# Two-head half-key attention slots, single products and output eighths, weight sums on VectorE, and a ring of query columns in a paged-attention kernel

## The chip, the cores and the metric

The kernel runs on one core of a Trainium2 chip. The metric is the device time of one launch in microseconds, as a median over runs. The engines are TensorE (PE; its weight loads are PEld), VectorE (DVE), ScalarE (ACT), GpSimd (POOL), and SyncE (SP), whose queue issues most of the DMA transfers.

## The reference

Two residual layers follow each other. The first is a 32x32 mix of the sequence rows of each batch, chosen by a condition. The second is paged attention with grouped heads. All is float32.

```python
B, S, HID = 64, 32, 512          # batches, new tokens of each, width
D, HQ, HK = 128, 32, 8           # head width, query heads, key/value heads
PAGES, PSIZE, NPP = 64, 32, 16   # cache pages, tokens of a page, pages of a batch

x = x + einsum('bct,bcd->bdt', x, weights[condition])          # layer 1

q, k, v = x @ Wq.T, x @ Wk.T, x @ Wv.T                         # layer 2, by heads
q, k = rope(rmsnorm(q, q_norm_w), pos), rope(rmsnorm(k, k_norm_w), pos)
k_all = concat([k_cache[block_table], k]); v_all = concat([v_cache[block_table], v])
scores = q @ k_all.T / sqrt(D)       # 512 cached keys (valid where < cache_seqlens), 32 new
o = softmax(scores) @ v_all          # four query heads share a key/value head
x = x + o @ Wo.T
```

## The kernel before

The work is 32 steps. Steps 0 to 15 are the sixteen groups of four batches (BT = 4, that is 128 rows) for the first four key/value heads, steps 16 to 31 the same groups for the other four. A step `n` runs over its four batches `bt` and, in each, over four slots `g`. So it has sixteen slots, `slot = bt * 4 + g`. In a slot of the kernel before, one key/value head `g` of one batch is worked on, with its four query heads times 32 tokens as 128 columns and all 512 cached keys.

In every slot TensorE computes the `scores` (L828: four 128x128 products), ScalarE makes the exponentials (L839), and TensorE computes the `values` of the slot before (L889: four 128x129 products, the last column being the sum of weights). After each second head VectorE adds the new tokens' part (L907), takes the reciprocal (L909) and scales into a tile `o` (L910); `turn` (L920) transposes it in 32x32 blocks into `ot`. VectorE copies the keys of a head from their pages into `kh` (`head_keys`, L821), `KH` = 3 slots ahead. SP loads the sixteen key pages of a batch (`load_k`, L321), two batches ahead. GpSimd gathers the values, one chunk of 128 keys at a time, by indirect DMA into one of three `raw` tiles (`fetch`, L348), and ScalarE copies them, scaled by 0 or 1 for validity, into the value tile (`mask_v`, L361).

At the head of a step come the new tokens' own scores (`new_scores`: L849, exponentials `pn` L857) in slot 0 and their values (`new_values`: L873, copied by ScalarE into `nv`, L881) in slots 1 and 3.

Between these a plan, written out by hand, puts pieces of work at (step, slot):

- The projections. From step 4 on, the q, k and v of two steps (a `Pair`, `s0` even and `s1` odd) are made together while the two steps before them run, by a scheme with seven products instead of eight (`products`, L687). A set `k` covers two projection blocks; sets 0 and 2 are made in the even step, set 1 in the odd one. Each set comes in four pieces (`p1_p6`, `p5_p2`, `p3_p7`, `p4_last`), two products in a piece but the last. The scheme needs sums of weights: `sums_w` and `sums_w4` make them on VectorE (L656 to L667) for the first pair of each half, store them to DRAM as `sums_d`, and `load_sums` (L674) brings them back for every later pair. The pieces add with VectorE (L703) and hand each result to `finish`, which queues it.
- The norm of a queued result: `square_next` (ScalarE squares 512 columns, L465) and `norm_next` (VectorE: product with the rotation table L475, sum of squares L482, plus epsilon L483, two more products L489, add L495, scaling L497; GpSimd the power -1/2, L485), then `turn_rows` (VectorE transpose L517, GpSimd stores the row block to `heads_d`, L521). `norm_slots` lists the slots at which results are taken from the queue.
- `spread` (L530) brings a step's query and key columns back from `heads_d`, in four transfers for the first three batches (`q_cols`, one buffer) and four for the last (`q_last`, two buffers).
- The output projection of the step before (`out_proj`, L767): sixteen 128x512 products, in quarters, at slots 5, 7, 9 and 10 from step 4 on (`out_parts`).
- The inputs of a later pair (`x1_a` loads, `x1_c` mixes, `x1_b` transposes) in the first half; in the second half `load_x` brings back what was kept.

Product, output, new-token and mixing banks share four PSUM buffers (`pp`), scores have two, values two. On SP, TensorE and, in the whole of this run, on every engine, instructions stay in the order in which the program writes them. An instruction that waits therefore holds back all that stands behind it on its engine; SP's transfers too leave in program order.

Of the kernel before, what the change touches and what calls it, by code (L numbers as in the profile page):

```python
# [51 lines left out]
KH = 3  # L52
# [7 lines left out]
def cond_resid_paged_attention_kernel(  # L60
# [118 lines left out]
    def other_half(by):  # L179
# [10 lines left out]
        for kind in "qk"  # L190
    }
    sums_d = [
        [
            dram.tile([P, 3, 2 * 512], F32, tag=f"sums_d{hh}{k}", name=f"sums_d{hh}{k}")
            for k in range(3)
        ]
        for hh in range(NHH)
    ]
# [10 lines left out]
    def steps_of(exact, pools):  # L209
# [15 lines left out]
        else:  # L225
# [7 lines left out]
        v_bufs = [  # L233
            wpool.tile([P, VC, GH, D + 1], F32, tag=f"v{i}", name=f"v{i}_{uid}")
            for i in range(2)
        ]
# [7 lines left out]
        if exact:  # L244
            rows = wpool.tile([P, 4, GH + 1, P], F32, tag="rows", name=f"rows_{uid}")
        q_cols = wpool.tile([P, BT - 1, GH + 1, P], F32, tag="q_cols", name=f"q_cols_{uid}")
        q_last = [
            wpool.tile([P, GH + 1, P], F32, tag=f"q_last{i}", name=f"q_last{i}_{uid}")
            for i in range(2)
        ]  # L250
# [56 lines left out]
        def load_k(hh, b, first_pages):  # L307
            k_raw = kv.tile([P, NPP, GH, PSIZE], F32, tag="k_t", name=f"k_t_{hh}_{b}_{uid}")

# [10 lines left out]
            def load_page(j):  # L320
                ins = nc.sync.dma_start(  # L321
                    k_raw[:, j, :, :].rearrange("p g r -> p (g r)"),
                    kt[hh, bass.ds(page[j], 1)].rearrange("o d e -> (o d) e"),
                )
                if exact:
                    r, c = j % BT * PSIZE, j // BT
                    ins = nc.sync.dma_start(
                        v_bufs[b % 2][r : r + PSIZE, c, :, 0:D],
                        vc.rearrange("(p r h) (g d) -> p h r g d", r=PSIZE, h=NHH, g=GH)[
                            bass.ds(page[j], 1), hh  # L330
                        ].rearrange("o r g d -> (o r) g d"),
                    )
                last_k[:] = [ins.ins]

            for j in range(first_pages):
                load_page(j)
            return k_raw, [lambda j=j: load_page(j) for j in range(first_pages, NPP)]
# [20 lines left out]
        def mask_v(b, c, raw):  # L358

            ok = valid[:, b, c : c + 1]  # L360
            nc.scalar.activation(v_bufs[b % 2][:, c, :, 0:D], raw, AF.Copy, scale=ok)  # L361

        def mask_ones(b):
            nc.gpsimd.tensor_copy(
                v_bufs[b % 2][:, :, :, D], valid[:, b, :].unsqueeze(2).to_broadcast([P, VC, GH])
            )
# [8 lines left out]
        def x1_a(st):  # L375

            tag, bufs = "acc", 2 if exact else 1
            if 0 < st.n < 6 and not exact:
                tag, bufs = "sums", 2
            elif st.n and not exact:  # L380
                tag = ("u2", "u3")[st.n % 2]
# [81 lines left out]
        def squares(pp, name):  # L463
            sq = work.tile([P, 4, D], F32, tag="w2", name=f"sq_{name}", bufs=1)
            nc.scalar.activation(  # L465
                sq.rearrange("p h d -> p (h d)"), pp, AF.Square, scale=1.0 / math.sqrt(D)
            )
            return sq

        def norm_rope(st, pp, name, kind, sq, to=None):  # L470
# [10 lines left out]
            ms = small.tile([P, 4], F32, tag="ms", name=f"ms_{name}")  # L481
            nc.vector.tensor_reduce(ms, sq, AX.X, ALU.add)  # L482
            nc.vector.tensor_scalar_add(ms, ms, EPS)  # L483
            rs = small.tile([P, 4], F32, tag="rs", name=f"rs_{name}")
            nc.gpsimd.tensor_tensor(rs, ms, minus_half, ALU.pow)  # L485

# [21 lines left out]
        def columns(st, bt):  # L508
            return q_last[st.n % 2] if bt == BT - 1 else q_cols[:, bt]
# [13 lines left out]
        def spread(st, b0, b1):  # L523


            src = heads_d[st.n].rearrange("k (b d) i c -> k d b (i c)", b=BT)
            to = q_last[st.n % 2].unsqueeze(1) if b0 == BT - 1 else q_cols
            to = to.rearrange("p b i c -> p b (i c)")
            for k in range(4):
                nc.sync.dma_start(to[k * S : (k + 1) * S], src[k][:, b0:b1, :])  # L530
# [25 lines left out]
        def normed(st, i, pp, name, kind, sq):  # L556

            if by_tensor(st):
# [12 lines left out]
                norm_rope(st, pp, name, kind, sq, to)  # L571
            else:
                turn_rows(st, i, norm_rope(st, pp, name, kind, sq))

        def to_columns(st, i, copy=nc.scalar.copy):
# [3 lines left out]
            n = BT - 1  # L579
            copy(q_cols[:, :, i, :].rearrange("p b (h s) -> p b h s", h=4), p4[:, 0:n])  # L580
            copy(columns(st, n)[:, i, :].rearrange("p (h s) -> p h s", h=4), p4[:, n])
# [43 lines left out]
        def pair_x(pair):  # L625
            pair.x = work.tile([P, 7, 2, P], F32, tag="x", name=f"x_{pair.name}", bufs=1)
# [3 lines left out]
        def load_x(pair):  # L630
            for i, st in enumerate(pair.both):
                nc.sync.dma_start(st.x1t.rearrange("p c q -> p (c q)"), x1t_d[st.t])
# [18 lines left out]
        made = {}  # L651

        def sums_w(hh, k):


            b11, _, b12, b22 = halves(hh, k)  # L656
            nc.vector.tensor_tensor(b12, b12, b11, ALU.subtract)
            t2, t3 = (sums_tile(f"t{i}_{hh}{k}") for i in (2, 3))
            nc.vector.tensor_tensor(t2, b22, b12, ALU.subtract)
            nc.vector.tensor_tensor(t3, t2, b11, ALU.subtract)  # L660
            made[hh, k] = t2, t3

        def sums_w4(hh, k):
            for i, t in enumerate(made[hh, k]):
                nc.sync.dma_start(sums_d[hh][k][:, i, :], t)
            t2 = made[hh, k][0]
            nc.vector.tensor_tensor(t2, halves(hh, k)[1], t2, ALU.subtract)  # L667
            kept.append(lambda: nc.sync.dma_start(sums_d[hh][k][:, 2, :], t2))
            return t2

        def load_sums(pair, k, i):

            t = sums_tile(f"t{i + 2}_{pair.name}_{k}")
            nc.sync.dma_start(t, sums_d[pair.hh][k][:, i, :])  # L674
            pair.t[k, i] = t

        def products(pair, k, first, late_v):
# [5 lines left out]
            flat = lambda t: t.rearrange("p h d -> p (h d)")  # L683

            def product(bank, i, w, start=False):
                for c in range(2):
# [3 lines left out]
                        w[:, c * 512 : (c + 1) * 512],  # L690
# [17 lines left out]

            t = {}

            def p1_p6():
                t[2] = made[pair.hh, k][0] if first else pair.t[k, 0]
                b11, t["b21"], t[1], t["b22"] = halves(pair.hh, k)
                t["a"], t["b"] = bank("pa"), bank("pb")
                product(t["a"], A11, b11, True)
                t["z"] = temp("z")
                nc.scalar.copy(t["z"], t["a"])
                product(t["b"], S2, t[2], True)
                t["u2"] = temp("u2")
                add(t["u2"], t["b"], t["z"])  # L720
                if first:
                    t[4] = sums_w4(pair.hh, k)

            def p5_p2():
                t["c"] = bank("pc")
                product(t["c"], S1, t[1], True)
                t["u3"] = temp("u3")
# [409 lines left out]
        for pair in pairs:  # L1137
            pair.t = {}
# [329 lines left out]
```

## Time and profile before

| | |
|---|---|
| median of 3 runs | 2241.11 us (2234.92 to 2241.31) |
| profiled execution | 2247.31 us, span 2245.5 us |
| mean granted TensorE clock | 0.975 |
| DMA traffic | 479.18 MB, mean 213 GB/s |
| start of step 4, by its first `psn` record | 367.7 us |
| start of step 30 | 2125.7 us |

The profile is one execution. A busy time is the union of an engine's instructions. In a row of groups the columns are the line, engine, operation, output and inputs with their shapes, the count, the busy time and the mean of one in ns, then the idle time just before and what ended it. A row of waits has the waiting line, what released it, the total, the number of times and the longest. A row of the timeline has the start, the length, the instruction, and in brackets the idle time before it. A float32 matmul of 512 columns stands in the records as two, and so do the others but the transposes.

### The profile page before, as it was taken

To read this page: it belongs to the slowest core of one execution; us is meant where nothing else is said; L and a number is where in the kernel's file an instruction comes from. 1 tells how busy PE (TensorE), PEld (TensorE's weight loads), DVE (VectorE), ACT (ScalarE), POOL (GpSimd) and SP (SyncE) were. 2 spreads that over 40 slices of the span, in tenths; PEclk is the share of its full clock that TensorE was granted. 3 is DMA by queue.
4 is the path that set the end of the run, shared out by engine and by line. 5 is a ranking of instruction groups with operands and counts; after the bars stand their busy time and mean duration, and the time that the engine had idled before them with its cause. 6 is when DMAs were issued, how large, how long until landed. Compare 5 with 4: busy or idle time off the path is not lost.

```text
span 2245.5 us, 42014 instructions
## 1 busy us (share of the span) xinstructions
PE 2118.6 (94%) x12804; PEld 1491.4 (66%) x12804; DVE 1420.8 (63%) x3142; ACT 879.6 (39%) x1604; POOL 910.5 (41%) x1090
## 2 busy tenths in 40 slices
PE   7999888999999999898899989999999999999998
PEld 4766646676667667666566666766676676766675
DVE  5566665775657667576665656757576665667632
ACT  3444324343444424443234333434443344443442
POOL 3344444344444444443334443434434333444431
PEclk9999988999999999999999999999999999999999
DMA  8766656777777777788667987677777767777672
GB/s 250 186 179 189 173 168 207 221 213 219 214 229 227 216 221 210 224 274 250 188 197 233 252 251 215 203 218 224 225 225 225 214 199 227 235 222 224 199 203 86
DMA packets 424539, 479.18 MB, mean 213 GB/s; under 512 B 57104, under 2 KB 323728, under 8 KB 424304
## 3 DMA queue, kind: packets, MB, share of 16 engines
q1 hardware_dynamic: 366240, 291.99, 45.0%
q0 software_dynamic: 55168, 180.27, 26.6%
q10 hardware_dynamic: 2896, 4.14, 0.5%
q8 instruction: 105, 1.72, 0.3%
q14 instruction: 130, 1.06, 0.2%
HBM read 406.71 MB, written 69.47 MB: 212 GB/s over the span
## 4 chain that ended last, share of the span: by engine, by line
PE 70%; DMA 10%; DVE 5%; issue 5%; SPq 4%; POOL 3%; ACT 1%; DVEq 0%; POOLq 0%; ACTq 0%
PE pout_x L767 16%; PE po_x L889 15%; PE ps_x L828 15%; PE pb_x L687 8%; PE pc_x L687 6%; PE pa_x L687 6%; SPq L321 3%; DMA k_t_x<-in_kt_dram 3%; DMA raw_x<-in_vc_dram,v_row 3%; PE pp_q_x L458 1%; DMA t_x<-sums_d 1%; PE pnv_x L873 1%; POOL raw_x L348 1%; POOL rs_q_x L485 1%; PE psn_x L849 1%
## 5 line engine op out<-in xcount | busy, mean ns | idle before, releaser
L348 POOL DMA_INDIRECT raw_x<-in_vc_dram,v_row x512 | 517.7, 1011 | 458.8 <-ACT v_x L361 348.0
L889 PEld LDWEIGHTS po_x<-v_x,pr_x 128*128 128x128 f32 x4088 | 528.4, 194 | 178.0 <-issue 152.7
L839 ACT ACTIVATE pr_x<-ps_x 128x512 f32<-128x512 f32 x511 | 303.6, 594 | 725.9 <-PE ps_x L828 721.1
L889 PE MATMUL po_x<-v_x,pr_x 128*128 128x129 f32 x4088 | 560.5, 281 | 19.0 <-ACT pr_x L839 13.3
L767 PE MATMUL pout_x<-wo_x,ot_x 128*128 128x512 f32 x1024 | 459.4, 592 | 0.0
L828 PE MATMUL ps_x<-q_cols_x,kh_x 128*128 128x128 f32 x3064 | 417.2, 280 | 42.1 <-DVE rot_q_x L444 21.2
L821 DVE COPY kh_x<-k_t_x 128x512 f32<-128x512 f32 x506 | 214.2, 430 | 360.5 <-PE ps_x L828 171.8
L361 ACT ACTIVATE v_x<-raw_x,valid 128x512 f32<-128x512 f32 x512 | 365.8, 718 | 171.3 <-DMA raw_x<-in_vc_dram,v_row 166.9
L828 PEld LDWEIGHTS ps_x<-q_cols_x,kh_x 128*128 128x128 f32 x3064 | 384.3, 197 | 45.4 <-issue 44.6
L767 PEld LDWEIGHTS pout_x<-wo_x,ot_x 128*128 128x128 f32 x1024 | 186.5, 190 | 194.7 <-issue 194.6
L485 POOL TENSOR_TENSOR rs_q_x<-ms_q_x,minus_half 128x4 f32<-128x4 f32 x128 | 142.6, 1114 | 334.2 <-DVE ms_q_x L483 333.4
L521 POOL DMA_DIRECT2D heads_d<-rows_x x150 | 125.6, 838 | 311.2 <-DVE rows_x L517 258.7
L687 PE MATMUL pb_x<-t_x,x_x 128*128 128x512 f32 x432 | 203.5, 593 | 2.3 <-DMA t_x<-sums_d 1.3
L907 DVE TENSOR_TENSOR nv_x<-po_x,nv_x 128x258 f32<-128x258 f32 x256 | 106.1, 415 | 114.8 <-PE po_x L889 109.3
L687 PEld LDWEIGHTS pb_x<-t_x,x_x 128*128 128x128 f32 x432 | 79.0, 190 | 89.6 <-issue 83.5
L828 PE MATMUL ps_x<-q_last_x,kh_x 128*128 128x128 f32 x1024 | 136.0, 276 | 0.0
L828 PEld LDWEIGHTS ps_x<-q_last_x,kh_x 128*128 128x128 f32 x1024 | 125.5, 193 | 0.0
L910 DVE TENSOR_TENSOR o_x<-nv_x,rden 128x256 f32<-128x256 f32 x256 | 110.0, 430 | 8.7
L687 PE MATMUL pc_x<-wq_x,x_x 128*128 128x512 f32 x224 | 107.3, 602 | 8.4 <-DVE u_x L703 8.4
L687 PE MATMUL pa_x<-wq_x,x_x 128*128 128x512 f32 x224 | 110.4, 617 | 0.0
L497 DVE TENSOR_TENSOR rope_q_x<-rope_q_x,rs_q_x 128x512 f32<-128x512 f32 x120 | 83.1, 692 | 27.0 <-POOL rs_q_x L485 16.1
L495 DVE TENSOR_TENSOR rope_q_x<-rope_q_x,ropeu_q_x 128x512 f32<-128x512 f32 x128 | 88.6, 692 | 4.4
(185 smaller groups left out, 1998.4 us busy)
## 6 DMA issues: line engine op xcount, KB each, us to landing
k_t_x<-in_kt_dram SPq DMA_DIRECT2D x2048, 64.0 KB
t_x<-sums_d SPq DMA_DIRECT2D x108, 512.0 KB
heads_d<-rows_x POOLq DMA_DIRECT2D x150, 256.0 KB
q_cols_x<-heads_d SPq DMA_DIRECT2D x120, 240.0 KB
q_last_x<-heads_d SPq DMA_DIRECT2D x120, 80.0 KB
sums_d<-t SPq DMA_DIRECT2D x18, 512.0 KB
raw_x<-in_vc_dram,v_row POOLq DMA_INDIRECT x512
wo_x<-in_wo_dram SPq DMA_DIRECT2D x32, 256.0 KB
```

Source lines behind the costliest of these rows:

```text
L348: nc.gpsimd.indirect_dma_start(out=raw.rearrange("p g d -> p (g d)"), out_offset=None, in_=vc, in_offset=bass.IndirectOffsetOnAxis(ap=v_ro ...
L361: nc.scalar.activation(v_bufs[b % 2][:, c, :, 0:D], raw, AF.Copy, scale=ok)
L485: nc.gpsimd.tensor_tensor(rs, ms, minus_half, ALU.pow)
L521: nc.gpsimd.dma_start(heads_d[st.n][:, :, i, :].rearrange("k p c -> p k c"), part)
L687: nc.tensor.matmul(bank, pair.x[:, i, c, :], w[:, c * 512 : (c + 1) * 512], start=start and c == 0, stop=c == 1, skip_group_check=not start,)
L767: nc.tensor.matmul(st.po, st.ot[:, i, :], wt["o", st.hh, i // 4][:, i % 4, :], start=(i == 0), stop=(i == QH - 1),)
L821: last["dve"] = nc.vector.tensor_copy(k, ba.k_raw[:, :, g, :]).ins
L828: nc.tensor.matmul(ps[:, c, :], ba.k[g][:, c * P : (c + 1) * P], queries(ba, g), start=True, stop=True,)
L839: last["act"] = nc.scalar.activation(pr, ps, AF.Exp, scale=SCALE).ins
L889: nc.tensor.matmul(ba.po[:, g % 2, :], ba.pr[g][:, c, :], ba.v_t[:, c, g, :], start=(c == 0), stop=(c == VC - 1),)
L907: nc.vector.tensor_tensor(t, ba.po, t, ALU.add)
L910: nc.vector.tensor_tensor(ba.o[:, both, :], t[:, :, 0:D], rd.unsqueeze(2).to_broadcast([P, 2, D]), ALU.mult,)
```

## The change

The kernel keeps what it computes and takes these parts apart differently:

- A slot of attention is two heads by half the keys (`part_of(j)`: heads `g`, `g+1`, half `j % 2`). The number of products is the same; values of two heads accumulate over two slots.
- Keys are loaded by half batches (eight pages, `load_half`) in the first two slots of a batch, into four buffers of half the size. `KH` is 4.
- Each product of a set is a piece of its own; so are the sums of weights `t2`, `t3`, `t4`, which VectorE makes anew for every pair. `sums_d` and its transfers are gone. `shift_w` makes the one sum that stays in place.
- The output projection is in eighths at slots 3 to 10 (in steps 1 to 3 bunched into two slots).
- Squares are four ScalarE instructions with an accumulated sum each; GpSimd adds epsilon; both a slot before the norm. `norm_slots` is new.
- The query columns are a ring of five batches (`q_ring`), loaded one batch at a time by one transfer of 128 partitions.
- The value tile is one ring tensor; `o` is gone, the result is scaled in place in `nv`; the second half of `new_values` moves from slot 3 to slot 2; one value chunk is copied in every slot.

```diff
-KH = 3
+KH = 4
+HP = NPP // 2
...
+        def load_k(hh, b, half):
+            if half == 0:
+                pages_of[hh, b] = page_numbers(b)
+            page = pages_of[hh, b]
+            k_raw = kv.tile([P, HP, GH, PSIZE], F32, tag="k_t", ..., bufs=4)
+            for j in range(HP):
+                nc.sync.dma_start(k_raw[:, j, :, :]..., kt[hh, bass.ds(page[half * HP + j], 1)]...)
+            return k_raw
...
-            nc.scalar.activation(
-                sq.rearrange("p h d -> p (h d)"), pp, AF.Square, scale=1.0 / math.sqrt(D)
-            )
+            for h in range(4):
+                nc.scalar.activation(
+                    sq[:, h, :], pp[:, h * D : (h + 1) * D], AF.Square,
+                    scale=1.0 / math.sqrt(D), accum_out=ms[:, h : h + 1],
+                )
+            nc.gpsimd.tensor_scalar(ms, ms, EPS, None, ALU.add)
+            nc.gpsimd.tensor_tensor(rs, ms, minus_half, ALU.pow)
...
-            nc.vector.tensor_reduce(ms, sq, AX.X, ALU.add)
-            nc.vector.tensor_scalar_add(ms, ms, EPS)
...
+            return q_ring[:, bt if exact else (st.n * BT + bt) % (BT + 1)]
...
+        def spread(st, bt):
+            nc.sync.dma_start(
+                columns(st, bt).rearrange("p i c -> p (i c)"),
+                heads_d[st.n].rearrange("k (b d) i c -> b k d (i c)", b=BT)[bt],
+            )
...
+            def t2():
+                t[2] = sums_tile(f"t2_{name}")
+                nc.vector.tensor_tensor(t[2], w(B22), w(T1), ALU.subtract)
+            def t3():
+                t[3] = sums_tile(f"t3_{name}")
+                nc.vector.tensor_tensor(t[3], t[2], w(B11), ALU.subtract)
+            def t4():
+                nc.vector.tensor_tensor(t[2], w(B21), t[2], ALU.subtract)
...
+            for c in range(2):
+                for i in range(2):
+                    nc.tensor.matmul(ps[:, c, i, :], ba.k[j][:, i, c, :], queries(ba, g + i), ...)
...
+                set_of(pair, 0, n,
+                    {3: "t2 1", 4: "2", 5: "6", 6: "5 t3", 7: "3 t4", 8: "7", 9: "4"})
+                set_of(pair, 1, n,
+                    {10: "t2", 11: "1", 12: "6 2 t3", 13: "5 t4", 14: "7 3", 15: "4"})
+                set_of(pair, 2, n + 1,
+                    {4: "t2 1", 5: "2 t3", 6: "6 t4", 7: "7", 8: "4", 11: "5", 13: "3"})
+                spread_of(s0, n + 1, (10, 10, 11))
+                ahead[n + 1, BT - 1].append(lambda st=s0: spread(st, BT - 1))
+            spread_of(s1, n + 2, (5, 7, 9, 13))
...
+        norm_slots = (5, 8, 9, 10, 14, 15), (1, 3, 7, 10)
...
+                where = range(3, 11) if n else ()
...
+                    if g < 2 and this.n + 2 < NHH * NT * BT:
+                        batch_of(this.n + 2).load_half()
```

In the slot lists a digit is one product of the set, `t2`, `t3` and `t4` are the sums of weights.

## The prediction

> **What bounds the kernel now.** I read the page's busy shares first, then TensorE's waits, then the same counts by stage, and last the timeline at the places where TensorE stood.
>
> ```profile
> PE 2118.6 (94%) x12804; PEld 1491.4 (66%) x12804; DVE 1420.8 (63%) x3142; ACT 879.6 (39%) x1604; POOL 910.5 (41%) x1090
> ```
>
> TensorE (PE) is the bound: it idles 2245.5 - 2118.6 = 127 us. The waits say on whom:
>
> ```profile
> PE ps_x L828 <- DVE rot_q_x L444: 21.2, 4, 5.8
> PE pnv_x L873 <- ACT pn_x L857: 17.6, 7, 5.2
> PE po_x L889 <- ACT pr_x L839: 13.3, 9, 4.1
> PE ps_x L828 <- DVE kh_x L821: 11.6, 4, 5.6
> PE pc_x L687 <- DVE u_x L703: 8.9, 2, 8.4
> PE pp_q_x L458 <- ACT x1t_x L409: 8.5, 1, 8.5
> ```
>
> Columns: total, times, longest. A few long gaps, then, not a steady drip. The rows by stage (step 3; steps 9 and 10; steps 21 and 22; the boundary of steps 19 and 20; a stretch inside step 20) show where:
>
> ```profile
> 264.50:367.70 103.20, 80.67 (x424) 54.12 (x423) 69.94 (x142) 33.07 (x59) 44.69 (x49) 0.89 0.56 174
> 714.10:850.60 136.50, 131.31 (x805) 92.58 (x805) 90.83 (x203) 57.32 (x103) 60.14 (x77) 0.97 0.74 220
> 1542.00:1672.70 130.70, 127.00 (x789) 89.56 (x788) 86.39 (x190) 52.45 (x96) 52.81 (x61) 1.00 0.75 221
> 1458.00:1474.60 16.60, 11.01 (x124) 10.11 (x122) 9.00 (x22) 6.95 (x13) 6.64 (x8) 0.91 0.99 288
> 1480.00:1530.00 50.00, 50.00 (x243) 31.59 (x242) 32.58 (x70) 17.45 (x31) 18.67 (x21) 1.00 0.68 202
> ```
>
> Columns: length, then PE, PEld, DVE, ACT, POOL busy, granted clock, DMA share, GB/s. Inside a step TensorE is full at clock 1.00 with the DMA engines at 0.68; at the boundary from an odd to an even step it has work for 11 of 16.6 us and the DMA engines stand at 0.99. There, eight slots hold only scores and values, so keys and values are asked for fastest just where column and weight-sum loads come too. Three such stalls:
>
> ```profile
> 1471.70 0.72 ACT L361 ACTIVATE v_x<-raw_x,valid 128x512 f32<-128x512 f32 x1 [7.21 <-DMA raw_x<-in_vc_dram,v_row]
> 1473.45 1.25 PE L873 MATMUL pnv_x<-vn_x,pn_x 32*128 32x129 f32 x16 [5.17 <-ACT pn_x L857]
> 1474.62 2.09 PE L889 MATMUL po_x<-v_x,pr_x 128*128 128x129 f32 x8
> ...
> 787.80 0.43 DVE L821 COPY kh_x<-k_t_x 128x512 f32<-128x512 f32 x1 [10.23 <-DMA acc_d<-acc_x]
> 788.38 2.05 PE L828 MATMUL ps_x<-q_cols_x,kh_x 128*128 128x128 f32 x8 [5.19 <-DVE rot_q_x L444]
> ...
> 299.10 1.23 DVE L667 TENSOR_TENSOR t<-wq_x,t 128x1024 f32<-128x1024 f32 x1 [11.39 <-DMA sums_d<-t]
> 302.35 2.07 PE L687 MATMUL pc_x<-wq_x,x_x 128*128 128x512 f32 x2 [8.43 <-DVE u_x L703]
> ```
>
> First: ScalarE's value copy waits for a gather, the exponentials queue behind it, TensorE behind them, and the next group takes 2.09 us where it takes 1.05 elsewhere (half clock). Second: VectorE's key copy waits for keys. The named rows store and table product are innocent (it is a wait for several); the key loads stood behind them on SP. Third: VectorE may not overwrite a weight sum before its store to DRAM has left.
>
> **The floor.** By start-to-start times in the filled stretches, eight 128-wide records take 0.89 us and one 512-wide record 0.43. A pair of steps has 32 slots x 1.78 = 57.0, new-token parts 4.6, output 64 x 0.43 = 27.5, products 84 x 0.43 = 36.0: 125.1 us; with the mixing of the first half's inputs 2.6 more, 127.7. The step starts (first psn records) put the 13 pairs of steps 4 to 29 at 1758 us against a floor of 1639: 119 over, that is 8 to 9 us in most pairs and 24 in pair 14/15, where new weight sums are made. Step 2 is 88.3 against 79.7, step 3 103.2 against 71.1: 41 over. Here a rule of the Trainium skill speaks against the change having much to win or lose at this end: "Trainium Kernel Development and Optimization" (Performance Expectations) calls matmul busy time a bad measure of the distance to the roofline and LDWEIGHTS busy the good one. By LDWEIGHTS' 66% some 750 us would be open; by the start-to-start floor 160 us in steps 2 to 29. I take the trace: in 1480 to 1530 the weight loads fill 31.59 us of 50 and TensorE still takes nothing more.
>
> **The change, part by part.** TensorE's instructions are the same in number and shape, so its floor stays; only waits can change.
>
> *Placing.* Products go one by one into slots 3 to 15 of even and 4 to 13 of odd steps, output eighths (two 512-wide products, 1.71 us) into slots 3 to 10 of both. The run of bare slots falls from eight (odd 12 to even 3) to six, with one product among them at odd 13: 15.9 us of TensorE work from odd 12 to even 2.
>
> *Traffic.* 108 loads and 18 stores of weight sums of 512 KB go: 66 of 479 MB. At the boundary they, and the two old copies of columns (8 issues, now 4 spread from odd 10 to 12), stood in SP's queue ahead of keys. Left in those 15.9 us: seven slots of keys and values (3.6 MB), two column loads (0.65 MB), the output store: 4.5 MB, 285 GB/s. The boundary row reached 288, so this fits with nothing to spare; prefetch helps, and I charge 1.5 us a pair.
>
> *Keys.* Half batches: a key copy needs eight pages, not sixteen, and is made four slots ahead, not three. The load for batch n+2 waits for copies made in batch n-1, so SP no longer stands on VectorE (198 us of SP's waits for L821 copies). The 5.2 us stalls of the first half (5, with about 2 us of slow clock each) should go.
>
> *Columns in a ring.* Each quarter is loaded 4 to 6 slots before use, after its slot's last reader; nothing on the path, bounds 0 and +1 us a pair (a row store that lands late); 0 taken.
>
> *VectorE.* Weight sums: 3 x 14 x 3 + 6 = 132 instead of 24, so 108 x 1.225 = +132 us. Squares' sums leave: 160 x (0.677 + 0.172) = -136. Total unchanged at 1.42 ms, but placed anew:
>
> ```profile
> L659 DVE TENSOR_TENSOR t<-wq_x 128x1024 f32<-128x1024 f32 x4 | 4.9, 1225 | 0.1
> L482 DVE TENSOR_REDUCE ms_q_x<-sq_q_x 128x4 f32<-128x512 f32 x128 | 86.7, 677 | 3.4 <-ACT sq_q_x L465 3.4
> L465 ACT ACTIVATE sq_q_x<-u_x 128x512 f32<-128x512 f32 x56 | 35.3, 630 | 122.2 <-DVE rope_q_x L495 69.0 <-DVE u_x L703 53.2
> L157 ACT ACTIVATE ang<-ang 128x128 f32<-128x128 f32 x6 | 1.8, 293 | 0.0
> ```
>
> A norm is 0.69 + 0.75 + 0.69 + 0.69 + 0.71 = 3.5 us. Even 12 to odd 3 asks of VectorE four norms (14), five product sums (3.4), two weight sums (2.4), eight key copies (3.4), four value ends (4), turns (1.4): 28.6 us against TensorE's 28. Walking it slot by slot, the fourth product of the set (even 15) waits 0.4 us for its bank and odd 1 and 2 another 0.8: 1.2 us a pair.
>
> *ScalarE.* A square becomes four of 128 columns with a sum each: nearest row 0.293, so 1.17 for 0.63; bounds 0.25 and 0.5 each. In odd 0 to 2 ScalarE then has 10 us (three exponentials and copies 3.9, pn 0.6, eight nv copies 3.1, two squares 2.3) for TensorE's 7.1; the following slot hides all but about 1 us a pair (at 0.5 us each: 2.5). Ninety us more in total hide behind TensorE.
>
> *GpSimd.* 160 additions of 128x4 (0.27, by its 128x16 copy) hide in its 59% idle. Here the skill speaks against the change: "SBUF — State Buffer" (Who interferes with whom) says a VectorE instruction with two SBUF inputs contends with a GpSimd one that reads SBUF, and the 108 new sums are such. By the trace L495 (two SBUF inputs, 692 ns) costs what L475 (one from PSUM, 0.68 us) costs, and gathers have a median of 977: 0 added. By the rule, up to 108 x 1.2 = 132 us of GpSimd's time, of which only the slots even 12 to odd 3 could reach the path: up to 2 us a pair. I take 0 and keep 2 for the range.
>
> *The o buffer* goes and the result is scaled in place: the same 0.43 us; nv copies now wait for the turn in slot 0, within 0.3 us of when they would start: counted above.
>
> **Sum.** Left over the floor: 1.5 + 1.2 + 1 = 3.7, say 4 us a pair, 13 x 4 + 4 for the two pairs with shifts = 56 against 119: -63. Steps 2 and 3: no store to wait for (37.5 us of VectorE's idle), sums spread; but norms, sums and products keep VectorE at 63 of 71 us in step 3: 5 and 8 us left against 41: -28. Opening and tail: 0. Together -91: 2154.5 us of span, 2156.3 with the 1.8 us around it; the median of before lies 6.2 under its profiled run (2247.31), so 2150.
>
> **Rivals.**
> (a) *Much smoother*, 4 us a pair becomes 1 to 2 and step 3 has no stall: another -40, 2110. For it: inside a step TensorE is full already.
> (b) *VectorE or the DMA engines take the boundary's place.* 28.6 against 28 and 285 against 288 leave nothing; 3 us more of either in each pair gives 13 x 3 = +39, with 8 more in step 3: 2197. Against it: VectorE has 15.8 us for 12 of work from odd 10 to 15, where it can catch up.
> (c) *The gather behind the row store*, the slower side. On GpSimd a row store waits for the norm's transpose and the next gather stands behind it. At even 15 my walk ends the norm 20.8 us after even 12; the gather lands 4.1 to 6.5 us after issue (1468 to 1474), and its copy is due at odd 2, near 27. If VectorE is 2.5 to 5 us later than I have it, ScalarE stands at even 15's and odd 1's gathers, each 5.2 + 2 us: 14.4 a pair against 9 now, 13 x 5.4 - 28 = +42, 2283. Below that lag nothing happens. Against it: norms no longer wait for GpSimd's power (333 us of its waits), being squared a slot ahead.
>
> **Numbers.** Main 0.60 (own range 2110 to 2190), (a) 0.12, (b) 0.17, (c) 0.08, and 0.03 for gains eaten exactly. A measurement of this kernel tells 0.3% (7 us) from no change. Faster 0.88, same 0.03, slower 0.09. Range 2095 to 2215.
>
> **Right or wrong.** Right: step-pair periods near 129 to 132, no PE gap over 3 us after step 4, granted clock 0.99 in the pair rows, VectorE near 1420 and ScalarE near 970 busy, 413 MB. Wrong: VectorE's waits for PE vanish while PE waits for u, z or kh (b); ScalarE's v copy waits for gathers at odd 2 to 4 with row stores before them (c); a square of 128 over 0.5 us.

## The result and the profile after

The changed kernel takes 2216.7 us (median of 5 runs, 2214.81 to 2219.98), the kernel before 2234.92 us beside it (5 runs): ratio 0.9913, 95% interval 0.989 to 0.9937. It is faster by 0.9% where 4% was forecast, and its time lies just above the stated range.

By the starts of steps (first `psn` records) the span went from 2245.5 to 2216.7 us like this: opening to step 2 176.2 to 178.2 us (+2.0), steps 2 and 3 191.5 to 186.3 (-5.2), steps 4 to 29 1758.0 to 1718.5 (-39.5), steps 30, 31 and the end 119.8 to 133.7 (+13.9). Forecast were 0, -28, -63 and 0.

The page's busy shares after:

```profile
PE 2109.8 (95%) x12804; PEld 1484.9 (67%) x12804; DVE 1425.6 (64%) x2930; ACT 958.3 (43%) x2706; POOL 1006.3 (45%) x1250
```

VectorE and ScalarE are where the prediction put them (1420 and 970), and traffic is 413.14 MB as forecast. TensorE still idles 107 us. On whom, say its waits (total, times, longest):

```profile
PE psn_x L866 <- DMA q_ring_x<-heads_d: 50.6, 13, 12.0
PE pb_x L677 <- DVE u_x L693: 13.1, 11, 3.2
PE po_x L908 <- ACT pr_x L856: 9.1, 6, 3.0
PE pp_q_x L465 <- ACT x1t_x L416: 7.9, 1, 7.9
```

The first row stood at 1.5 us before (`psn` for `q_last`) and is now the largest of either kernel: a step's first scores wait for their query columns. The waits that the change was to remove (for `kh`, `rot_q`, `pn`) have left the top of the list. SP's waits show the same transfer from the other side, first in the kernel before, then in the changed one:

```profile
SPq L321 <- DVE kh_x L821: 198.2, 59, 10.0
...
SPq L321 <- DMA q_cols_x<-heads_d: 12.6, 17, 1.5
...
SPq L324 <- DMA q_ring_x<-heads_d: 204.9, 78, 6.4
SPq L324 <- DVE kh_x L836: 101.4, 51, 11.8
SPq L536 <- PE ps_x L845: 98.3, 19, 9.0
```

SP's waits for VectorE's key copies halved (198.2 to 101.4 us), but its key loads (L324) now stand 205 us behind column loads, for 12.6 us before. The rows by stage (length, PE, PEld, DVE, ACT, POOL busy, clock, DMA share, GB/s) for steps 6 and 7, steps 14 and 15, steps 22 and 23, and the end:

```profile
513.20:648.50 135.30, 130.90 (x805) 92.16 (x806) 92.94 (x191) 61.92 (x172) 66.16 (x86) 0.99 0.63 186
1046.00:1174.10 128.10, 127.54 (x793) 90.02 (x795) 92.26 (x181) 57.78 (x166) 62.53 (x71) 1.00 0.68 207
1569.50:1696.80 127.30, 127.06 (x789) 89.71 (x788) 89.26 (x178) 57.66 (x165) 61.24 (x71) 1.00 0.64 191
2083.00:2216.70 133.70, 107.82 (x739) 81.64 (x738) 37.23 (x98) 42.72 (x79) 27.59 (x35) 0.91 0.45 133
```

Where no column is late, a pair takes 127.3 us against a floor of 125.1: better than the 129 forecast. So the mechanism works and something else takes the time back. Step 2 grew from 88.3 to 98.4 us, steps 4 and 5 together from 134.0 to 148.7 and the end from 119.8 to 133.7; of TensorE's waits for columns, 9.9, 10.8 and 18.8 us lie there. The end shows it best, with TensorE busy for 107.82 of 133.70 us at clock 0.91. The timeline there, SP first and then TensorE (start, length, instruction, idle before it):

```profile
2126.85 0.58 SPq L536 DMA_DIRECT2D q_ring_x<-heads_d  x1
2129.24 11.17 SPq L324 DMA_DIRECT2D k_t_x<-in_kt_dram  x16
2140.51 0.59 SPq L536 DMA_DIRECT2D q_ring_x<-heads_d  x1
...
2148.14 1.91 PE L866 MATMUL psn_x<-q_ring_x 128*32 128x128 f32 x26 [12.05 <-DMA q_ring_x<-heads_d]
2149.98 2.09 PE L908 MATMUL po_x<-v_ring_x,pr_x 128*128 128x129 f32 x8
2151.86 1.38 PE L845 MATMUL ps_x<-q_ring_x,kh_x 128*128 128x128 f32 x8
```

Step 31 began at 2128.25; the last quarter of its columns is asked for at 2140.51, behind sixteen key loads, and TensorE has it at 2148.14. The group after it takes 2.09 us for the usual 1.05: the granted clock stands at 0.50 from 2148.1 to 2152.0, after the gap.

**On how many DMA engines the transfer runs.** The columns are the only packets of 2560 bytes in the trace's DMA records, so a quarter (128 of them) can be timed where it goes alone. The mean of engines at work is the sum of its packets' times over its length:

| columns of one batch | alone, median | DMA engines at work, mean |
|---|---|---|
| before: four transfers of 32 partitions | 2.5 us | about 7 |
| after: one transfer of 128 partitions | 5.3 us | 3.4 |

The source of the one transfer is `b k d (i c)` at one `b`, so its slowest dimension is `k`, of 4. The Trainium skill has the rule ("DMA: Bandwidth & Descriptors", Why a DMA increments its semaphore by 16 and not by 1): a transfer is spread over the largest number of engines up to 16 that divides the slowest dimension of both its patterns. For 128 and 4 that is four; the records show 3.4 in the mean. The packets under way at one moment say it more sharply: of the time in which any column packet is under way, it is four for 50% in the changed kernel and more than five for under 1%, while in the kernel before it is 16 or more for 24%. (For 32 and 32 the rule gives sixteen.) The prediction did not apply it.

### The profile page after: what moved, and what is told of

Its sections match the earlier page's. It is cut to its first block, busy times and chain, and to the rows that moved or that the text cites. A ratio compares the mean times of both kernels' runs of the same rounds, so it can differ in the third digit from the quotient of the medians.

```text
span 2216.7 us, 42993 instructions
## 1 busy us (share of the span) xinstructions
PE 2109.8 (95%) x12804; PEld 1484.9 (67%) x12804; DVE 1425.6 (64%) x2930; ACT 958.3 (43%) x2706; POOL 1006.3 (45%) x1250
## 2 busy tenths in 40 slices
DMA packets 403042, 413.14 MB, mean 186 GB/s; under 512 B 51728, under 2 KB 318352, under 8 KB 402800
## 4 chain that ended last, share of the span: by engine, by line
PE 74%; DMA 12%; DVE 5%; SPq 3%; issue 3%; POOL 2%; ACT 1%; ACTq 0%; DVEq 0%; POOLq 0%
PE pout_x L773 17%; PE po_x L908 16%; PE ps_x L845 16%; PE pb_x L677 8%; DMA q_ring_x<-heads_d 6%; PE pa_x L677 6%; DMA k_t_x<-in_kt_dram 4%; PE pc_x L677 4%; SPq L324 2%; PE pnv_x L890 2%; PE pp_q_x L465 2%; PE psn_x L866 1%; POOL rs_q_x L483 1%; POOL raw_x L357 1%; DMA raw_x<-in_vc_dram,v_row 1%
## 5 line engine op out<-in xcount | busy, mean ns | idle before, releaser
L908 PEld LDWEIGHTS po_x<-v_ring_x,pr_x 128*128 128x128 f32 x4088 | 527.3, 193 | 176.2 <-issue 150.9
L908 PE MATMUL po_x<-v_ring_x,pr_x 128*128 128x129 f32 x4088 | 553.4, 278 | 9.3 <-ACT pr_x L856 9.1
L845 PE MATMUL ps_x<-q_ring_x,kh_x 128*128 128x128 f32 x4088 | 548.6, 277 | 1.6 <-ACT q_ring_x L591 1.6
L845 PEld LDWEIGHTS ps_x<-q_ring_x,kh_x 128*128 128x128 f32 x4088 | 504.3, 193 | 21.3 <-issue 15.5
L370 ACT ACTIVATE v_ring_x<-raw_x,valid 128x512 f32<-128x512 f32 x512 | 368.7, 721 | 100.3 <-DMA raw_x<-in_vc_dram,v_row 71.1
L677 PE MATMUL pb_x<-t_x,early 128*128 128x512 f32 x504 | 241.5, 602 | 14.2 <-DVE u_x L693 13.1
L677 PEld LDWEIGHTS pb_x<-t_x,early 128*128 128x128 f32 x504 | 86.6, 192 | 79.3 <-issue 61.7
L922 DVE TENSOR_TENSOR nv_x<-nv_x,rden 128x256 f32<-128x256 f32 x256 | 111.4, 435 | 8.7
L677 PE MATMUL pc_x<-wq_x,early 128*128 128x512 f32 x224 | 105.5, 593 | 1.1 <-DVE u_x L693 1.1
L677 PE MATMUL pa_x<-wq_x,early 128*128 128x512 f32 x224 | 105.3, 593 | 0.0
L866 PE MATMUL psn_x<-q_ring_x 128*32 128x128 f32 x1024 | 45.7, 300 | 50.6 <-DMA q_ring_x<-heads_d 50.6
```

What stands on the lines that cost most here:

```text
L370: nc.scalar.activation(v_of(b)[:, c, :, 0:D], raw, AF.Copy, scale=ok)
L677: nc.tensor.matmul(bank, pair.x[:, i, c, :], by[:, c * 512 : (c + 1) * 512], start=start and c == 0, stop=c == 1, skip_group_check=not start,)
L845: nc.tensor.matmul(ps[:, c, i, :], ba.k[j][:, i, c, :], queries(ba, g + i), start=True, stop=True,)
L908: nc.tensor.matmul(ba.po[:, i, :], ba.pr[j][:, c, i, :], ba.v_t[:, 2 * half + c, g + i, :], start=(half == 0 and c == 0 and i == 0), stop= ...
L922: nc.vector.tensor_tensor(t[:, :, 0:D], t[:, :, 0:D], rd.unsqueeze(2).to_broadcast([P, 2, D]), ALU.mult,)
```

## Experiments

Each comparison ran on one chip beside the kernel before, whose median lay between 2235 and 2249 us from one comparison to the next; so ratios to before are compared. The theory: the one column transfer of 128 partitions, on few engines, takes back most of the forecast gain. Rivals: the gain is not there (the boundary is bound by something else), or the ring's order, not its transfers, is at fault.

**Four transfers for a quarter.**

```diff
-            nc.sync.dma_start(columns(st, bt)..., heads_d[st.n]...[bt])
+            src = heads_d[st.n].rearrange("k (b d) i c -> b k d (i c)", b=BT)[bt]
+            for k in range(4):
+                nc.sync.dma_start(to[k * S : (k + 1) * S], src[k])
```

> The changed kernel with one edit: each quarter of the query columns is loaded by four transfers of 32 partitions instead of one of 128 (same bytes, 360 more issues on SP). Theory A (a single column transfer moves on only 3 to 4 of the 16 DMA engines, 5.3 us a quarter, and the key loads queue behind it): TensorE's waits of psn for q_ring fall from 50.6 us to under 10, the last two steps from 133.7 us to about 121, the whole to about 2155 us (2140 to 2175). Rival B (the DMA engines or VectorE are full at the step boundary, and the columns only show it): the wait moves to kh or pr, 2205 to 2217. Rival C (SP's queue is the bound, 360 issues at 0.3 to 0.6 us more): 2217 or more.

2163.39 us, ratio 0.9664 (0.9622 to 0.9705), against 0.9913: inside the theory's range and far from both rivals. The waits of TensorE and of SP:

```profile
PE psn_x L866 <- DMA q_ring_x<-heads_d: 19.6, 5, 7.8
...
SPq L324 <- DMA x1t_d<-early: 41.9, 11, 6.8
```

A quarter takes 2.6 us on about 7 engines. The waits for columns fall from 50.6 to 19.6 us (under 10 were expected), and SP's wait behind columns leaves its first rows. The whole is 53 us by the medians, 56 by the ratios. Of the 53.3 us between the two profiled spans, 31.0 are these waits, 9.1 the waits for exponentials (`po <- pr`, above), which are gone, and 12.7 TensorE's busy time, which falls from 2109.8 to 2097.1 us as the granted clock rises from 0.978 to 0.987. TensorE waits for keys in neither kernel.

**The store of `x1t` from SP, not ScalarE.** In the first half ScalarE issues the store of its own `x1t` (L421). The timeline of the changed kernel, with TensorE's row beneath:

```profile
508.41 0.33 ACTq L421 DMA_DIRECT2D x1t_d<-early  x1
508.78 0.72 ACT L370 ACTIVATE v_ring_x<-raw_x,valid 128x512 f32<-128x512 f32 x1 [5.10 <-DMA k_t_x<-in_kt_dram]
...
510.04 1.48 PE L908 MATMUL po_x<-v_ring_x,pr_x 128*128 128x129 f32 x8 [2.97 <-ACT pr_x L856]
```

The copy at 503.09 ends at 503.7, the issue comes out at 508.41, and ScalarE does nothing between; TensorE then waits 2.97 us for the exponentials. ScalarE stands so six times, 25.5 us in all, by its waits. I took it for a cost of its own.

```diff
-            if st.n or exact:
+            if in_slots:
+                kept.append(lambda: keep_x1t(st, nc.sync))
+            elif st.n or exact:
                 keep_x1t(st, nc.scalar)
```

> As the run with four column transfers, and the store of the transposed inputs of a pair leaves from SP's queue two slots later instead of from ScalarE's queue (12 stores in the first half). If ScalarE's wait in front of that store (5.1 us before 508 us, with TensorE 3.0 us idle) is a cost of its own, the pairs of steps 6 to 11 fall from about 135 us to 131 and the whole by another 10 to 15 us. If it only waited because the column transfers held the queue, no difference over 3 us to the run with four transfers.

With this and the four transfers: 2152.21 us, ratio 0.9614 (0.9574 to 0.9654), 11 us less. But the 25.5 us are not what it saves. With the four transfers alone ScalarE no longer stands there (copy at 489.51 with 0.59 us, issue at 490.12), and TensorE's waits for `pr` are already gone: in the changed kernel that stall came along with the column transfers on few engines. What was left, and goes here, is the row of SP's key loads behind the store, 41.9 us in the fence above. So the first expectation met the number for another reason. That this row is what the 11 us are is read from the rows; the place of the store, two slots later, changed with its queue. By the starts of steps it is worth 7.5 us in steps 4 to 15 and 4.6 in steps 2 and 3. The pairs of steps 6 to 9 now take 131.6 us, those of steps 12 to 15, in which no inputs are mixed any more, 127.6, and most second-half ones 126.7.

**The transfer of 128 partitions alone, in the kernel before.** `spread` of before loads each batch by one transfer of four groups of 32 rows.

```diff
-            for k in range(4):
-                nc.sync.dma_start(to[k * S : (k + 1) * S], src[k][:, b0:b1, :])
+            for b in range(b0, b1):
+                nc.sync.dma_start(columns(st, b)..., src[b])
```

> The kernel before with one edit: the columns of a step are loaded by one transfer of 128 partitions for each batch instead of four of 32 partitions for three batches and four for the last (4 issues instead of 8, same bytes, same places in the queue). Theory A: a step's columns take about 20 us to land instead of 8, at both step boundaries: slower, by 5 to 12 us in each of 28 steps, 2235 + 140 to 330. Rival B (placing in the queue matters, not the transfer's shape): 2235 within 10 us.

2442.88 us, ratio 1.0908 (1.0861 to 1.0954), 205 us slower. TensorE's and SP's waits:

```profile
PE psn_x L847 <- DMA q_cols_x<-heads_d: 64.9, 23, 5.7
PE psn_x L847 <- DMA q_last_x<-heads_d: 63.7, 15, 5.6
...
SPq L321 <- DMA q_cols_x<-heads_d: 129.9, 48, 5.8
```

The same two rows as in the changed kernel, about 5.5 us a quarter on about 3.3 engines. It costs more here, and columns come more in bursts: in 22 of 30 steps the four quarters follow each other without a break, 20.9 us together, in the changed kernel in 14. That the ring's spreading softens the cost is my reading of this, not tested apart.

**Two transfers of 64 partitions**, in the changed kernel: a slowest dimension of 2.

```diff
+            for k in (0, 2):
+                nc.sync.dma_start(to[k * S : (k + 2) * S], src[k : k + 2])
```

> The changed kernel (2216.7 us) with each column quarter in two transfers of 64 partitions (two groups of 32 rows of the source each) in place of one of 128. Theory (the outer dimension of the source decides over how many DMA engines a transfer is spread: four in one transfer, two in each of these, 6 to 7 in all when four transfers of 32 partitions each go): a quarter is not faster than with one transfer, 5 us or more of packet time on four engines or fewer, TensorE's waits for columns stay at 40 us or more, 2210 to 2260 us. Rival (smaller transfers are faster, whatever their outer dimension): half way to the four-way kernel, a quarter in 3 to 4 us, waits of 30 us or less, 2175 to 2200 us.

2590.99 us, ratio 1.1515 (1.1475 to 1.1556).

```profile
PE psn_x L866 <- DMA q_ring_x<-heads_d: 304.0, 39, 22.0
...
SPq L324 <- DMA q_ring_x<-heads_d: 316.3, 116, 5.3
```

A quarter takes 9.7 us on 1.7 engines. "Smaller transfers are faster" is dead; the number of engines follows the slowest dimension: 3.4 for 4, 1.7 for 2. My size was far too low (2260 us at most), since I took the two transfers for additive. They are not: two packets are under way for 72% of the time in which any is, three or more for 5%. The skill's same passage says that SP's transfers use the lowest-numbered engines, so that both would share the same two; the records do not name the engine. Another layout of `heads_d`, from which one transfer could use them all, was not tried.

**The last quarter in an idle tile.** With a ring of five, a quarter waits for the slot of five batches earlier.

```diff
         def columns(st, bt):
+            if st is steps[-1] and bt == BT - 1 and not exact:
+                return early[...]
...
-            spread_of(s1, n + 2, (5, 7, 9, 13))
+            spread_of(s1, n + 2, (5, 7, 9, 6 if s1 is steps[-1] else 13))
```

> The kernel of the four-way column loads with the store from SP (2152.2 us), with one more edit: in the last step the last batch's columns go into the pair tile, which is idle by then, and are loaded in slot 6 of step 30 and not into the ring in slot 13. Theory (what is left of the cost of the ring is its order: a quarter cannot be loaded before the slot of the batch five before it is free, so in the last step it comes 8 us late): the wait of psn for columns in step 31 (8.1 us, once) is gone, the half clock after it too, 2142 us (2138 to 2147). Rival (the load is late because SP's queue is long there, wherever it is put): 2152 (2149 to 2156).

Ratio 0.9562 (0.9529 to 0.9594), 2150.04 us where before took 2248.06: the fastest complete kernel here, and 0.5% below the kernel of ratio 0.9614 by the ratio, as expected, with intervals that overlap a little. Its page and waits:

```profile
PE 2087.2 (97%) x12804; PEld 1470.3 (69%) x12804; DVE 1427.0 (67%) x2930; ACT 957.0 (45%) x2706; POOL 1014.2 (47%) x1250
...
PE pb_x L681 <- DVE u_x L697: 11.9, 10, 3.2
PE pp_q_x L467 <- ACT x1t_x L416: 7.7, 1, 7.7
PE psn_x L870 <- DMA q_ring_x<-heads_d: 6.6, 4, 2.6
```

The 8.1 us wait of step 31 is gone. By steps: opening 172.6, steps 2 and 3 179.6, steps 4 to 29 1675.0, the end 114.0 us.

**What made the rest.** Three parts of the change were undone, each by itself. First, in the kernel of ratio 0.9614, output eighths two by two in slots 5, 7, 9, 10:

```diff
-                where = range(3, 11) if n else ()
+                where = (5, 5, 7, 7, 9, 9, 10, 10) if n else ()
```

> The kernel of the four-way column loads with the store from SP (2152.2 us), with the output eighths put two by two into slots 5, 7, 9 and 10, as the output quarters were before. Theory of placing (the gain comes from TensorE's own work filling more slots, so that fewer bare slots pull keys and values): slots 3, 4, 6 and 8 lose 1.7 us of cover each in both steps; with 1 to 2.5 us a pair lost, 2165 to 2185 us. Rival (only the bare run from odd 12 to even 3 matters, and the bunching leaves just one more bare slot there): 2150 to 2160 us.

Ratio 0.9699 (0.9665 to 0.9734): 0.85%, some 19 us or 1.5 us a pair of steps, as the theory of placing had it.

Second, in the same kernel, squares of 512 columns with sums and epsilon on VectorE:

> The kernel of the four-way column loads with the store from SP (2152.2 us), with the squares as before: one ScalarE instruction of 512 columns, their sums and epsilon by VectorE (160 x (0.677 + 0.172) = 136 us more for VectorE, about 90 us less for ScalarE). Theory (VectorE is level with TensorE from even 12 to odd 3, 28.6 against 28 us, so each of the four norms there that takes 0.85 us longer moves the end): up to 3.4 us a pair, 2170 to 2195 us, with waits of TensorE for u and of its banks. Rival (VectorE has room, ScalarE is what is short): 2140 to 2155 us.

Ratio 0.9678 (0.9645 to 0.971): 0.64%, some 14 us, at the low end of what was expected (the intervals overlap slightly). TensorE's wait that grew, against 11.8 us in 10 waits:

```profile
PE pb_x L675 <- DVE u_x L691: 24.2, 40, 3.5
```

Third, in the fastest kernel, `KH` of 3:

> The fastest kernel so far (ratio to before 0.956) with key copies made three slots ahead, not four. Theory (half batches of keys let SP go on without VectorE, but the copies still need the fourth slot where VectorE is level with TensorE): TensorE waits for kh at the boundary, 1 to 3 us a pair, ratio 0.962 to 0.974. Rival (the half batches alone do it): ratio 0.954 to 0.959.

Ratio 0.9582 (0.9557 to 0.9606): no difference that can be told from 0.9562, and the theory's 0.962 to 0.974 is ruled out. The fourth slot ahead buys nothing that shows here.

**Products bunched**, in the fastest kernel:

```diff
-                    {3: "t2 1", 4: "2", 5: "6", 6: "5 t3", 7: "3 t4", 8: "7", 9: "4"},
+                    {4: "t2 1 2", 6: "6 5 t3", 7: "3 t4", 8: "7 4"},
...
-                    {4: "t2 1", 5: "2 t3", 6: "6 t4", 7: "7", 8: "4", 11: "5", 13: "3"},
+                    {4: "t2 1 2 t3", 6: "6 t4 7", 8: "4", 11: "5 3"},
```

> The fastest kernel (ratio to before 0.956) with the products of two sets bunched: set 0 in even slots 4, 6, 7, 8 (2, 2, 1 and 2 products), set 2 in odd slots 4, 6, 8, 11 (2, 2, 1 and 2), so that even 3, 5, 9 and odd 5, 7, 13 have none and odd 11 is followed by seven bare slots. Theory of placing (the same as for the eighths, which cost 1 to 2 us a pair when bunched): 0.5 to 2 us a pair, ratio 0.959 to 0.970. Rival (slots 3 to 10 are covered by the eighths already, so single products there bring nothing): ratio 0.954 to 0.958.

Ratio 1.027 (1.0227 to 1.0314), far outside both expectations, with these waits of TensorE:

```profile
PE pb_x L681 <- DVE u_x L697: 50.3, 23, 4.0
PE pc_x L681 <- DVE vn_x L697: 28.3, 12, 2.6
PE pa_x L681 <- ACT z_x L722: 22.0, 26, 4.5
PE pb_x L681 <- DVE t_x L709: 13.9, 13, 2.3
```

Not bare slots but accumulation banks (the PSUM buffers in which products add up): product 2 goes on in the bank that ScalarE must first copy for `z`, 7 in the one that VectorE must first add, and with both in one slot TensorE stands waiting. One product a slot keeps these chains covered. This bunching is tighter than before's, which kept 1 and 2, and 6 and 7, in different slots; so its size is no measure of what the change gained over before.

**The weight sums.** In the kernel before, made by VectorE for every pair, with no loads:

```diff
-                which[place].append(lambda ...: load_sums(pair, k, i))
+                at(m, slots[0] - before, lambda ...: sums_w(pair, k, fresh))
```

> The kernel before with one part of the change alone: VectorE makes the sums of weights anew for every pair, nothing is stored to or loaded from DRAM for them (66 MB less; VectorE 132 us more), at the slots at which the first pair of each half makes them. If the traffic at the boundary is what costs there: the pairs fall from 135 to about 131 and steps 2 and 3 by 15 us: about 2175. If VectorE's place in slots 2 to 14 is the tighter: each pair gets some of the 24 us over the floor that pair 14/15 shows, 2235 to 2350. My reading: between, about 2220.

Ratio 1.0047 (1.0031 to 1.0064), so slower, where I had expected a gain. Its page:

```profile
PE 2127.9 (94%) x12804; PEld 1489.8 (66%) x12804; DVE 1545.4 (69%) x3250; ACT 878.4 (39%) x1604; POOL 958.9 (43%) x1090
```

VectorE's busy time rose from 1420.8 to 1545.4 us, SP's wait for key copies from 198 to 300. GpSimd's rose from 910.5 to 958.9 us with the same instructions, its gathers from 1011 to 1073 ns. The loss is not everywhere: steps 2 and 3 fell from 191.5 to 178.7 us, steps 4 to 29 rose from 1758.0 to 1779.6. Then the kernel before with neither loads nor new sums (its products read plain weight blocks, so it leaves out that part of the computation):

> The kernel before without the 108 loads of weight sums; from the second pair of each half on, the products that read a sum read a plain weight block of the same shape in its place (this part of the computation is changed). TensorE and VectorE do what they did, only DMA traffic goes (54 of 479 MB). Theory of the prediction (the boundary of an odd to an even step is bound by DMA traffic, 0.99 of 16 engines at 288 GB/s): the 8 to 9 us left in a pair shrink by 2 to 4 us, 2195 to 2220 us where before takes 2237. Rival (the stalls there come from the order of copies and gathers, and the traffic only looks full): 2228 to 2240.

Ratio 0.9957 (0.9929 to 0.9986), 10 us, nearer the rival. The boundary of steps 19 and 20 in this kernel, and then in the fastest one:

```profile
1431.50:1448.10 16.60, 12.55 (x132) 11.19 (x131) 8.97 (x22) 7.16 (x14) 6.60 (x8) 0.99 0.90 243
...
1383.90:1400.50 16.60, 15.73 (x166) 13.59 (x165) 8.15 (x22) 8.48 (x18) 6.93 (x9) 1.00 0.76 227
```

Without the sums' loads the DMA share falls from 0.99 to 0.90, but TensorE still has work for 12.55 of 16.6 us only (11.01 before). So the traffic of the sums was not the main limit of that boundary. And the fastest kernel without VectorE's sums, which leaves out the same part:

> The fastest kernel so far (four-way column loads, store from SP, last quarter in the idle tile; ratio to before 0.956) without VectorE's 132 sums of weights from step 4 on; the products read plain weight blocks of the same shape in their place (this part of the computation is changed). Theory (VectorE is level with TensorE at the boundary, as the squares put back on it suggest, 16 us for 112 to 136 us of work): 10 to 25 us less, ratio 0.945 to 0.952. Rival (what is left of VectorE's work is covered): ratio 0.954 to 0.958.

Ratio 0.9542 (0.9512 to 0.9571), not told apart from 0.9562: 138 us of VectorE's work (1427.0 to 1288.8; the edit takes out 126 sums) are all but covered once products and squares lie as they do. Beside the kernel with `KH` of 3, on the same chip, it is 7 us (2141.33 to 2134.01). By the starts of steps the pairs of steps 6 to 9 gain 2.5 us each (131.6 to 129.1), most second-half ones 0.2.

## Why the prediction was wrong

- *The failed step* is "Columns in a ring": "nothing on the path, bounds 0 and +1 us a pair (a row store that lands late); 0 taken". I counted issues (eight down to four) and due slots, and never on how many DMA engines the one that stayed would run: 5.3 us a quarter for 2.5. It measured 50.6 us of TensorE's waits, 205 us of SP's, and with the waits for `pr` and the slower clock 53 to 56 us of time; the wait for a ring slot at the very end was some 9 us more by the starts of steps, 12 by the ratio. The note about a late row store was the wrong bound: the transfer itself was late.
- *A second term missed* is ScalarE's store of `x1t`, before which SP's key loads wait: 11 us, as far as the rows tell. The prediction weighed the transfers that SP and GpSimd issue, and not those of ScalarE. Whether moving this store helps the kernel before too was not tried.
- *Opening and tail, 0 taken*: +2.0 and +13.9 as run, -3.6 and -5.8 once columns are mended ("mended" is here and below the kernel of ratio 0.9562). The tail's cost was the columns'.
- *The pairs, -63*: -39.5 as run, -83.0 mended. I left 4 us a pair over the floor; second-half pairs stand near 126.7, under 2 us over it: rival (a)'s size. Those of steps 6 to 9 keep 3.9, of which 2.5 go with VectorE's sums. The floor held: 127.06 us busy of 127.30 at clock 1.00. The Trainium skill's weight-load measure ("Trainium Kernel Development and Optimization", Performance Expectations) would still see 30% open there, with PEld at 89.71 us.
- *Why the boundary improves* was only part right. I charged it to traffic (285 of 288 GB/s); removing the sums' loads gave 10 us, and the mended boundary moves 227 GB/s. The bunched eighths (19 us) and the squares (14 us) show placing and VectorE's load to be at work. Half batches, two-head slots and `norm_slots` were not undone, so 50 or more us of the gain are not split among them.
- *Keys*: "SP no longer stands on VectorE" was wrong. The 101.4 us in the changed kernel were low while SP stood behind columns; in the mended one it stands 157.1 us on the key copies again. It costs nothing: TensorE's 11.6 us of waits for `kh` are gone all the same, with `KH` of 3 too.
- *VectorE level with TensorE*: right in part. Adding its sums alone slows before (GpSimd slows with them there, so the loss is not VectorE's for certain); putting the squares back costs 14 us; the swap keeps the total at 1425.6. But 138 us taken away are worth some 7: VectorE stands near the edge, not on the path. Rival (b), 2197, did not occur.
- *ScalarE*: 160 squares with their sums take 195.9 us for 99.0, so +0.61 each for 0.54 forecast. The total rose by 78.7 only, as its other instructions are busy for 18 us less.
- *GpSimd*: 0 added was too little. The rule of the skill that the prediction set aside ("SBUF — State Buffer", Who interferes with whom) shows on GpSimd: 108 more sums alone cost it 48 us in the kernel before, 0.45 each, and without the sums the fast kernel's GpSimd is busy for 970.9 us, where it is 1004.9 in the same kernel with `KH` of 3. The 48 us are about a third of the 132 reckoned as its most. VectorE's two-input add kept its 692 ns. With GpSimd at 45% no wait of TensorE points to it; 0 on the path was not shown wrong.
- *Rival (c)*: no; ScalarE's waits for gathers fell from 166.9 to 71.1 us.
- *Steps 2 and 3, -28*: -5.2, and -11.9 mended. Step 3 fell from 103.2 to 87.1 us; the sums made anew, alone in the kernel before, take it to 90.1, so the store of sums that held VectorE was rightly named. Step 2 rose from 88.3 to 92.5 even in the mended kernel. TensorE idles for 8.1 of these 92.5 us, 5.1 of them still for columns; why the rest did not gain stays open.

In all: -28.8 us of span as run for -91, and -104.3 mended (98 by the medians, 2248.06 to 2150.04). That the mended ratio, 0.956, is near the forecast one, 0.959, is partly luck, as terms cancel: the pairs gave 20 us more than forecast, the opening and the end 9 more, steps 2 and 3 16 less.

## What to carry to other kernels

Before merging DMA transfers into one, look at the slowest dimension of both access patterns and at how many DMA engines the packets really use: fewer instructions can mean a transfer twice as long, and everything behind it on its queue waits too. After a change, read the waits of the issuing queue beside those of TensorE; here one row of SP's list named the fault. Products that share an accumulation bank belong in different slots, with the other engine's read between them. A stretch in which an engine idles before its own DMA issue can have its cause on another engine's queue, so count the transfers of all queues.

## What the runs showed of the hardware

- Two transfers with a slowest dimension of 2 do not add up: 1.7 engines at work, 9.7 us for 320 KB.
- A sum that ScalarE takes along is an instruction of its own. In the groups of the changed kernel the 188 ns reads stand beside the 297 ns squares. Their records overlap; a square of 512 columns in four parts with sums takes 1.22 us of ScalarE for 0.62 in one:

```profile
L474 ACT ACTIVATE sq_q_x<-u_x 128x128 f32<-128x128 f32 x224 | 66.2, 297 | 128.5 <-DVE u_x L693 127.2 <-DVE rope_q_x L505 1.3
L474 ACT ACTIVATION_READ_ACCUMULATOR sq_q_x<-u_x 128x1 f32 x224 | 42.0, 188 | 0.0
```

- An engine that issues a transfer can stand in front of it: 4.7 us of ScalarE between its copy and the issue at 508.41. By the records of all fifteen issues of this store, ScalarE stood over 1 us in front of five in the changed kernel (2.0 to 8.8 us), of four with two transfers of 64 partitions (15.5 to 16.9) and of five in the kernel before with the transfer of 128 (3.6 to 12.2). In the kernel before as it was, and in the changed one with four transfers, all fifteen left 0.03 us after the work ahead of them. So in these runs it stands there only beside column transfers on few engines, though these are on SP's queue; why it does is not shown.
- VectorE's sums of two inputs slow GpSimd: 108 more of 128x1024 made it busy for 958.9 us instead of 910.5 with the same instructions, while VectorE's 128x512 add stayed at 692 ns.
